# Splitting the Fourier phase's small matmuls along the columns of the TensorE array, with b1's term as a further row

## The chip, the cores and the metric

The kernel runs on one core of one Trainium2 chip. The metric is the device time of one execution in microseconds (us), taken as the median of three runs. The engines are named as in the profile: PE (TensorE, matmul), PEld (its weight load), DVE (VectorE), ACT (ScalarE), POOL (GpSimd) and SP (SyncE, which issues nearly all transfers here).

## The reference

The input has 64 samples of 96 channels and 56 by 56 places. A first layer normalizes groups, makes a 7x7 kernel for every channel with a small MLP and convolves with it. The second layer is the one that matters here. For each sample it takes the 3136 places as tokens t, and computes:

```
h = relu(bn1(layernorm(t) @ w1.T))            # 3136 tokens x 192 channels
X = fft(h, axis=tokens)                       # ortho
xr = relu(X.real*rd - X.imag*idg + rb)        # rd, idg: diagonals of r and i
xi = relu(X.imag*rd + X.real*idg + ib)
y = ifft(xr + 1j*xi).real
t = t + bn2(y @ w2.T)
t = t + ffn(layernorm(t))                     # 96 -> 384 -> 96, products in fp8
```

## The kernel before

The convolution phase (`conv_layer`) runs first and leaves its result `x1` in DRAM. Then `fourier_layer` works through the 64 samples. Each sample passes three parts.

`front` goes through seven chunks of 448 tokens. It loads tokens (`t`), sums squares, multiplies by w1 (`w1c`), normalizes and applies the ReLU into `g`, and makes the first half of the transform with `dft1`. The result goes to DRAM (`turned`).

`middle` does what the change touches. It works on 30 frequencies of the first transform (29 of them used), in four batches of 8, 8, 8 and 6 (`k0` is the batch's first, `n` its number). `load` fetches `Y`, with 112 rows (real and imaginary parts of 56 places along w), up to eight frequencies and 192 channels. `group(q)` makes the transform over w with `dft2`. For q = 0 the channels are 0 to 127, and each frequency is one matmul with 128 columns of weights (Y is the operand that is loaded, dft2 the one that streams, 112 elements). For q = 1 they are channels 128 to 191, two frequencies side by side in the upper and lower 64 partitions, each a matmul of 64 columns. Frequency 0 of the whole transform gets b1's term: a second matmul, with `b1row` (one row) as weights and `dc` streaming, is accumulated onto the first. Several ACT, DVE and POOL steps then apply the complex product and the ReLUs and leave `CD0` and `CD1` (tiles of 120 columns: 56 values, 8 zeros, 56 values). `project` multiplies them by w2: `w2b` for q = 1 in the upper or lower 64 rows of the array, `w2a` for q = 0 with all rows. Both load 120 columns of CD as weights and stream the 96 columns of w2. They accumulate into two PSUM banks, one for each h. `over_k2` transforms back over the second index with `inv1`, and the result goes to DRAM.

`ending` transforms back over the first index with `inv2` (tile `U`), adds the residual, normalizes again, and runs the MLP (`W1T`, `W2T`) on chunks of 448.

The order of all this isn't written by hand. Every step is given to a `Plan` with a due time, an engine, a cost in us, what it reads and writes, and for PE a kind (how the array is tiled). `emit` plays these costs through as events and issues each step when it starts an engine in that play, earliest due time first, favouring a step of the kind that the engine has just done within a patience of 37.3, and charging 0.13 for a change of kind. The eight PSUM banks are given out in the same play: `ps` takes one and `big` takes two together. `Pinned` then holds every engine to the order in which its steps were issued, so all engines and SP's queue are in order.

Two steps carry the costs that the change edits:

```
pe(T - 429.9, (0.92 if q else 1.9) * ng / 8 + dc_, dft, ...)
pe(T - 226.2, 0.345 * n, project, ..., kind=("halves", "full"))
```

Almost every instruction is recorded under one line of a helper (L406), so rows in the profile are told apart by their tiles: `l_psum<-dft,Y` is the transform over w, `l_psum<-dc,b1row` b1's term, `l_psum<-w2b,CD` and `l_psum<-w2a,CD` the product with w2.

Of the kernel before, what the change touches and what calls it, by code (L numbers as in the profile page):

```python
# [118 lines left out]
def constants():  # L119

    h, k = place_of_h(), np.arange(K1)
    keep = (k < NK).astype(float)
    dft1 = np.zeros((2, 64, HALF, 64))
    inv2 = np.zeros((2, 2, K1, HALF, 2, S))
    weight = keep * np.where((k == 0) | (k == NK - 1), 0.5, 1.0)

    order = np.concatenate([k[at : at + 8][h::2] for at in range(0, K1, 8) for h in range(2)])
    for wp in range(2):
        for j in range(HALF):
            w = columns()[wp, j]  # L130
            th = 2 * np.pi * k[None, :] * (S * h[:, None] + w) / HW

            dft1[wp, :S, j, :K1] = np.cos(th) / S * keep
            dft1[wp, :S, j, K1 : 2 * K1] = -np.sin(th) / S * keep

            co, si = ((f(th) / S * weight).T[order] for f in (np.cos, np.sin))
            if j == 0:
                inv2[0, wp, :, j, wp], inv2[1, wp, :, j, wp] = co, -si  # L140
            else:
                sign = 1 - 2 * wp
                inv2[0, 0, :, j, wp], inv2[0, 1, :, j, wp] = co, -sign * si
                inv2[1, 0, :, j, wp], inv2[1, 1, :, j, wp] = -si, sign * co
    a = np.arange(S)
    ph = 2 * np.pi * (a[:, None] * a[None, :]) / S
    co, si = np.cos(ph), np.sin(ph)

    dft2 = np.block([[co, -si], [si, co]]).reshape(2, S, RI)[:, place_of_w()]


    inv1 = np.zeros((2, 64, HALF, 2))
    inv1[:, :S, :, 0] = co[:, :HALF]
    inv1[0, :S, :, 1], inv1[1, :S, :, 1] = si[:, :HALF], -si[:, :HALF]
    inv1[:, :S, 0, 1] = co[:, HALF]
    inv1 = np.concatenate([inv1.reshape(128, S), np.zeros((128, 64 - S))], 1)

    dc = np.zeros((1, RI))
    dc[0, 0] = S


    f = np.arange(32)
    there = (f <= L // 2).astype(float)
    th = 2 * np.pi * (a[:, None] - (S - 1) / 2) * f[None, :] / L
    fwd_y = np.zeros((2, 64, 2, 32))
    fwd_y[:, :S, 0] = np.cos(th) * there
    fwd_y[:, :S, 1] = -np.sin(th) * there


    g = np.arange(64)  # L170
    here = (g < L).astype(float)
    half = np.arange(HALF)
    th = 2 * np.pi * (half[:, None] - (S - 1) / 2) * g[None, :] / L
    cx, sx = np.cos(th) * here, np.sin(th) * here
    fwd_x = np.zeros((2, 64, 64))
    fwd_x[0, :S] = np.concatenate([cx, sx])
    fwd_x[1, :S] = np.concatenate([cx, -sx])

    inv_x = np.tile(fwd_x.transpose(2, 0, 1), (2, 1, 1))


    share = there * np.where((f == 0) | (f == L // 2), 1.0, 2.0) / L**2
    th = 2 * np.pi * f[:, None] * (half[None, :] - (S - 1) / 2) / L
    cy, sy = np.cos(th) * share[:, None], np.sin(th) * share[:, None]
    inv_y = np.stack([np.stack(v, 1) for v in ((cy, cy), (cy, -cy), (-sy, -sy), (-sy, sy))])


    d = np.arange(KS) - RAD
    spec = np.zeros((2, 2, 32, 4, 2, 2, 64))
    for q in range(4):  # L190
        for g_ in range(2):
            for p in range(2):
                for e in range(2):
                    fy = 8 * q + 4 * e + 2 * g_ + p
                    ph = 2 * np.pi * (fy * d[:, None, None] + g * d[None, :, None]) / L
                    ph = ph.reshape(KS * KS, 64)[PAIRS:]
                    spec[p, 0, : PAIRS + 1, q, g_, e] = np.cos(ph) * here * there[fy]
                    spec[p, 1, : PAIRS + 1, q, g_, e] = np.sin(ph) * here * there[fy]

    fold = np.zeros((2, 64, 2, 64))  # L200
    fold[:, :, 0] = fold[0, :, 1] = np.eye(64) / 2.0
    fold[1, :, 1] = -np.eye(64) / 2.0
    middle = np.zeros((3, 128))
    middle[2, [0, 64]] = 1.0
    group = np.kron(np.eye(ROWS // 3), np.full((3, 3), 1.0 / 3.0))
    mean = np.full((C, C), 1.0 / C)

    sel = np.zeros((4, 32, 4))
    sel[:, 0] = np.eye(4)
    named = dict(  # L210
        dft1=dft1.reshape(128, HALF, 64), sel=sel.reshape(128, 4), dft2=dft2.reshape(RI, RI), inv1=inv1[:TOK],
        inv2=inv2.reshape(4 * K1, HALF, RI), dc=dc, group=group, center=np.eye(C) - mean,
        fwd_y=fwd_y.reshape(128, 64)[:TOK], fwd_x=fwd_x.reshape(128, 64)[:TOK], inv_x=inv_x, inv_y=inv_y.reshape(128, S),
        spec=spec.reshape(128, 4, 2, 128), middle=middle,
        fold=fold.reshape(128, 128),
        ident=np.eye(128),
    )
    return {k: np.ascontiguousarray(v, np.float32) for k, v in named.items()}
# [993 lines left out]
def fourier_layer(tc, nc, x1, out, weights, con):  # L1212
# [8 lines left out]
    with ExitStack() as ctx:  # L1221
# [17 lines left out]
            return t  # L1239

        sel, dft1 = const("sel", [128, 4]), const("dft1", [128, HALF, 64])
        dft2, inv1 = const("dft2", [RI, RI]), const("inv1", [TOK, 64])
        dc, inv2 = const("dc", [1, RI]), const("inv2", [4 * K1, HALF, RI])
        eps = cp.tile([128, 1], F32, name="eps")
        nc.vector.memset(eps, 1e-5)
        over = cp.tile([C, 32], F32, name="over")
# [7 lines left out]
        for t in CDs[0] + CDs[1]:  # L1254
# [4 lines left out]
                "w1c", "nb1", "b1row", "w2a", "w2b", "bias2", "pa", "W1T", "W2T", "fb1", "fb2",  # L1259
            )  # L1260
        )

        def pe(when, cost, step, **kw):
            plan.add(when, "PE", cost, step, lag=PE_LAG, **kw)
# [153 lines left out]
        def middle(b, T, turned):  # L1418
# [4 lines left out]
            def batch(m, T):  # L1423
# [4 lines left out]
                    return (tag, "m", b, m, *more)  # L1428

                def load():  # L1430
                    v["Y"] = sbuf("Y", [RI, 8, H1], F32, f"Y{b}_{m}")
                    for r in range(2):
                        for half in range(2):
                            p = r * S + half * HALF
                            nc.sync.dma_start(
                                v["Y"][p : p + HALF, :n], rows[half, r, :, k0 : k0 + n]
                            )

                def group(q, T):
# [6 lines left out]
                    def dft():  # L1446
                        w["ps"] = bank(ps, 2 - q).rearrange("p (g x) -> p g x", x=128)
                        for g in range(ng):
                            for e in range(1 + q):
                                k = g if q == 0 else 2 * g + e  # L1450
                                lo, hi = (64 * e, 64 * e + 64) if q else (0, 128)
                                channels = slice(128 * q, 128 + 64 * q)
                                to_ = w["ps"][lo:hi, g, :RI]
                                nc.tensor.matmul(
                                    to_, v["Y"][:, k, channels], dft2,
                                    start=True, stop=k0 + k > 0,
                                )
                                if k0 + k == 0:
                                    nc.tensor.matmul(
                                        to_, b1row[:, channels], dc, start=False, stop=True  # L1460
                                    )
                        w["re"], w["im"] = w["ps"][:, :ng, :S], w["ps"][:, :ng, S:RI]

                    def act(key, src, func, **kw):
# [18 lines left out]
                    def minus():  # L1483
# [6 lines left out]
                    )  # L1490
                    CD = nm(f"CD{q}")
                    add = plan.add
                    dc_ = 0.4 if k0 == 0 else 0.0
                    pe(T - 429.9, (0.92 if q else 1.9) * ng / 8 + dc_, dft, r=[nm("Y")],
                       w=[ps, p, r2, t, w2, CD], kind=("columns2" if q else "full"))


                    add(T - 240.9, "ACT", 0.26 + 0.84 * e,
# [17 lines left out]
                def project():  # L1516

                    for h in range(2):
                        v["o", h] = bank(nm("ps", 0, h))[:TOK]


                    for g in range(n // 2):
                        for h in range(2):
                            half = slice(64 * h, 64 * h + 64)
                            nc.tensor.matmul(
                                v["o", h][:, g * C : (g + 1) * C], v[1][half, g], w2b[half],
                                start=g == 0, stop=False,
                            )
                    ks = [k for k in range(n) if k0 + k < NK]
                    for k in ks:  # L1530
                        g, h = k // 2, k % 2
                        nc.tensor.matmul(
                            v["o", h][:, g * C : (g + 1) * C], v[0][:, k], w2a,
                            start=False, stop=k + 2 not in ks,
                        )

                width = n // 2 * C

# [34 lines left out]
                    [nm(x, y, h) for h in range(2)]  # L1573
                    for x, y in (("ps", 0), ("E", 0), ("ps", 1), ("t2", 0))
                )
                pe(T - 226.2, 0.345 * n, project, r=[nm("CD0"), nm("CD1")], w=[*o, *E], kind=("halves", "full"))
                for h in range(2):
                    U = T + 15 + 2.0 * h
                    add(U - 239.2, "ACT", 0.17 + 0.042 * n, lambda h=h: keep(h),
# [304 lines left out]
```

## Time and profile before

| what | value |
|---|---|
| median of 3 runs | 6957.5 us (6955.31 to 6960.29) |
| span of the profiled execution | 6947.6 us |
| time of the profiled execution beside its span | not given apart; the median is 9.9 us over the span |
| one sample in the steady part of the Fourier phase | 65.42 us |
| busy over the span | PE 95%, PEld 63%, DVE 75%, ACT 63%, POOL 48% |
| mean granted TensorE clock | 0.978 |

The span is the time from the first to the last instruction of one profiled execution. Busy time is the union of an engine's instructions; matmuls overlap each other and their ends are modelled, so a count of passes and the distance between starts say more of PE than its busy share. A float32 matmul stands as two passes in the trace, so x16 is eight matmuls. PEld runs beside PE. A row of the timeline merges neighbouring instructions of the same tiles: it shows the start, the time to the last one's end, the tiles, the shapes and the number, and the idle time ahead of it where there was some.

### The profile page before, as it was taken

What the parts mean: (1) busy time and instruction counts of PE and PEld (TensorE: products, weight loads), DVE (VectorE), ACT (ScalarE), POOL (GpSimd) and SP (SyncE); (2) the same over time, 40 slices, a digit from 0 to 9 for tenths busy, and PEclk for the clock granted to TensorE, in tenths of its full rate; (3) what the DMA queues carried; (4) which work ended last, traced back from release to release, by engine and by line L of the source; (5) the groups of instructions that cost most, each with busy time, mean ns of one, the idle gap of its engine ahead of it and who ended that gap; (6) DMA issues with size and microseconds to landing.
All of it is one profiled execution on the core that took longest, in us unless ns stands there. A gap on an engine that the chain in (4) does not pass through costs nothing.

```text
span 6947.6 us, 180667 instructions
## 1 busy us (share of the span) xinstructions
PE 6579.9 (95%) x67027; PEld 4382.2 (63%) x67027; DVE 5231.0 (75%) x10600; ACT 4391.6 (63%) x10582; POOL 3307.1 (48%) x3604
## 2 busy tenths in 40 slices
PE   8999999999999998999999999999999999999997
PEld 3455555555555556777777777777777777777774
DVE  4555555555555543899999999999999999999997
ACT  3444444443443433777777777877878777777776
POOL 0221111112111221666666666666666666666666
PEclk9999999999999986999999999999999999999997
DMA  4677777777777776667777767767777777677664
GB/s 138 179 200 204 207 199 204 201 198 211 199 200 200 205 195 168 184 193 195 198 191 195 194 191 195 195 192 198 193 193 198 192 194 198 190 194 197 193 183 129
DMA packets 1328576, 1334.92 MB, mean 192 GB/s; under 512 B 756763, under 2 KB 1201758, under 8 KB 1320665
## 3 DMA queue, kind: packets, MB, share of 16 engines
q1 hardware_dynamic: 1325864, 1313.79, 69.1%
q8 instruction: 532, 8.72, 0.5%
q10 hardware_dynamic: 1833, 9.57, 0.4%
q14 instruction: 347, 2.84, 0.1%
HBM read 743.17 MB, written 579.63 MB: 190 GB/s over the span
## 4 chain that ended last, share of the span: by engine, by line
DVE 27%; PE 19%; ACT 8%; issue 5%; DMA 4%; SPq 1%; POOL 0%; DVEq 0%; POOLq 0%; ACTq 0%
PE l_psum L406 17%; DVE h L406 5%; DVE CD L406 5%; DVE g L406 4%; DVE mr L406 3%; DVE x L406 3%; DVE t L406 3%; ACT h L406 3%; ACT r L406 2%; DMA turned<-t 2%; DVE p L406 2%; DVE w L406 1%; ACT t L406 1%; ACT p L406 1%; PE s L406 1%
## 5 line engine op out<-in xcount | busy, mean ns | idle before, releaser
L406 POOL TENSOR_TENSOR t<-t,t 128x504 f32<-128x504 f32 (+1 forms) x392 | 489.9, 1253 | 2105.1 <-DVE t L406 2104.8
L406 PE MATMUL pm<-w0g,xT 128*126 128x512 f32 (+3 forms) x2450 | 1151.0, 611 | 3.0 <-ACT xT L406 3.0
L406 PEld LDWEIGHTS pm<-w0g,xT 128*126 128x126 f32 (+3 forms) x2450 | 442.2, 192 | 531.5 <-issue 523.4
L406 PE MATMUL l_psum<-dft,Y 112*128 112x112 f32 (+1 forms) x7552 | 738.7, 274 | 8.3 <-ACT E L406 1.7
L406 POOL TENSOR_TENSOR t<-t,y 96x448 f32<-96x448 f32 x448 | 500.2, 1117 | 479.0 <-DVE y L406 478.8
L406 PEld LDWEIGHTS l_psum<-dft,Y 112*128 112x128 f32 (+1 forms) x7552 | 650.3, 164 | 110.0 <-DVE g L406 32.8
L406 ACT COPY B<-s 120x504 f32<-120x504 f32 (+1 forms) x392 | 207.5, 580 | 801.4 <-PE s L406 734.6
L406 PE MATMUL l_psum<-w1c,t 96*56 96x193 f32 (+1 forms) x7168 | 690.5, 336 | 0.0
L406 ACT CAST h<-l_psum 128x448 f16<-128x448 f32 x1344 | 661.2, 550 | 11.3 <-PE l_psum L406 11.3
L406 ACT COPY t<-l_psum 128x384 f32<-128x384 f32 (+2 forms) x1408 | 614.0, 486 | 29.3 <-PE l_psum L406 23.2
L406 DVE SCALAR_TENSOR_TENSOR g<-l_psum,st,nb 120x192 f32<-120x192 f32 x1792 | 627.6, 402 | 4.8
L406 DVE TENSOR_TENSOR t<-s,W 128x504 f32<-128x504 f32 (+1 forms) x784 | 481.6, 672 | 186.9 <-PE s L406 186.8
L406 POOL TENSOR_TENSOR sq<-t 96x448 f32<-96x448 f32 x448 | 476.8, 1070 | 264.5 <-PE l_psum L406 223.2
L406 POOL TENSOR_TENSOR mr<-mr 128x112 f32<-128x112 f32 x896 | 499.2, 560 | 216.8 <-ACT mr L406 179.3
L406 POOL TENSOR_TENSOR nb<-t,nb 96x448 f32<-96x448 f32 x448 | 571.8, 1277 | 56.6 <-DMA nb<-norms 56.4
L406 ACT ACTIVATE h<-h,fb 128x448 f16<-128x448 f16 x896 | 593.7, 693 | 0.0
L406 POOL TENSOR_TENSOR sqb<-t 96x448 f32<-96x448 f32 x448 | 557.7, 1255 | 41.2 <-DVE t L406 25.7
L406 PEld LDWEIGHTS l_psum<-w1c,t 96*56 96x56 f32 (+1 forms) x7168 | 505.8, 136 | 37.9 <-ACT t L406 0.3
L406 PEld LDWEIGHTS s<-inv_y,V 64*126 64x126 f32 (+1 forms) x5488 | 357.8, 194 | 229.1 <-ACT B L406 100.5
L406 PE MATMUL s<-inv_y,V 64*126 64x56 f32 (+1 forms) x5488 | 395.8, 282 | 98.6 <-ACT B L406 50.3
L406 ACT ACTIVATE t<-l_psum,pa 128x224 f32<-128x224 f32 (+3 forms) x512 | 306.4, 610 | 254.9 <-PE l_psum L406 253.1
L406 DVE TENSOR_TENSOR x<-nb 96x448 fp8e5<-96x448 f32 x448 | 362.0, 808 | 124.3 <-POOL nb L406 121.9
(131 smaller groups left out, 14058.2 us busy)
## 6 DMA issues: line engine op xcount, KB each, us to landing
turned<-t SPq DMA_DIRECT2D x896, 180.0 KB
nb<-norms SPq DMA_DIRECT2D x448, 336.0 KB
Y<-turned SPq DMA_DIRECT2D x768, 168.0 KB
Y<-turn_x SPq DMA_DIRECT2D x768, 110.2 KB
turn_y<-B SPq DMA_DIRECT2D x768, 110.2 KB
V<-turn_y SPq DMA_DIRECT2D x336, 252.0 KB
U<-turned SPq DMA_DIRECT2D x896, 90.0 KB
t<-x SPq DMA_DIRECT2D x448, 168.0 KB
```

Of the source, the lines that this page charges most:

```text
L406: ins = issue(*args, **kw)
```

## The change

The transform for q = 0 becomes two matmuls of 64 columns for each frequency, one for channels 0 to 63 into PSUM partitions 0 to 63, one for 64 to 127 into the others; q = 1 stays as it was. b1's row is put into partition 112 of Y at its first frequency, and `dc` becomes the 113th row of dft2; for frequency 0 the matmul takes 113 rows and the accumulated second matmul goes. So that the row stays, Y is no tile of the pool any more but one of two constant tiles, `Ys`, used in turn, whose row is filled once at the start of the phase from ACT's queue. In `project` each matmul is cut into columns 0 to 63 and 64 to 119. The costs and kinds given to the plan follow; due times stay.

```diff
-    dft2 = np.block([[co, -si], [si, co]]).reshape(2, S, RI)[:, place_of_w()]
+    dft2 = np.block([[co, -si], [si, co]]).reshape(2, S, RI)[:, place_of_w()].reshape(RI, RI)
...
-        dft2=dft2.reshape(RI, RI)
+        dft2=np.concatenate([dft2, dc])
...
-        dft2, inv1 = const("dft2", [RI, RI]), const("inv1", [TOK, 64])
-        dc, inv2 = const("dc", [1, RI]), const("inv2", [4 * K1, HALF, RI])
+        dft2, inv1 = const("dft2", [RI + 1, RI]), const("inv1", [TOK, 64])
+        inv2 = const("inv2", [4 * K1, HALF, RI])
...
+        Ys = [cp.tile([RI + 1, 8, H1], F32, name=f"Y{e}") for e in range(2)]
+        for t in Ys:
+            nc.scalar.dma_start(t[RI:, 0], b1row)
...
-                    v["Y"] = sbuf("Y", [RI, 8, H1], F32, f"Y{b}_{m}")
+                    v["Y"] = Ys[(4 * b + m) % 2]
...
-                            for e in range(1 + q):
-                                k = g if q == 0 else 2 * g + e
-                                lo, hi = (64 * e, 64 * e + 64) if q else (0, 128)
-                                channels = slice(128 * q, 128 + 64 * q)
-                                to_ = w["ps"][lo:hi, g, :RI]
+                            for e in range(2):
+                                k = 2 * g + e if q else g
+                                at = 128 if q else 64 * e
+                                rows_ = RI + (k0 + k == 0)
                                 nc.tensor.matmul(
-                                    to_, v["Y"][:, k, channels], dft2,
-                                    start=True, stop=k0 + k > 0,
+                                    w["ps"][64 * e : 64 * e + 64, g, :RI],
+                                    v["Y"][:rows_, k, at : at + 64], dft2[:rows_],
+                                    start=True, stop=True,
                                 )
-                                if k0 + k == 0:
-                                    nc.tensor.matmul(
-                                        to_, b1row[:, channels], dc, start=False, stop=True
-                                    )
...
-                    dc_ = 0.4 if k0 == 0 else 0.0
-                    pe(T - 429.9, (0.92 if q else 1.9) * ng / 8 + dc_, dft, r=[nm("Y")],
-                       w=[ps, p, r2, t, w2, CD], kind=("columns2" if q else "full"))
+                    pe(T - 429.9, 0.21 * ng, dft, r=[nm("Y")], w=[ps, p, r2, t, w2, CD],
+                       kind="columns2")
...
+                    cut = [slice(0, 64), slice(64, TOK)]
                     for g in range(n // 2):
                         for h in range(2):
                             half = slice(64 * h, 64 * h + 64)
-                            nc.tensor.matmul(
-                                v["o", h][:, g * C : (g + 1) * C], v[1][half, g], w2b[half],
-                                start=g == 0, stop=False,
-                            )
+                            for to in cut:
+                                nc.tensor.matmul(
+                                    v["o", h][to, g * C : (g + 1) * C], v[1][half, g, to],
+                                    w2b[half], start=g == 0, stop=False,
+                                )
...
-                        nc.tensor.matmul(
-                            v["o", h][:, g * C : (g + 1) * C], v[0][:, k], w2a,
-                            start=False, stop=k + 2 not in ks,
-                        )
+                        for to in cut:
+                            nc.tensor.matmul(
+                                v["o", h][to, g * C : (g + 1) * C], v[0][:, k, to], w2a,
+                                start=False, stop=k + 2 not in ks,
+                            )
...
-                pe(T - 226.2, 0.345 * n, project, r=[nm("CD0"), nm("CD1")], w=[*o, *E], kind=("halves", "full"))
+                pe(T - 226.2, 0.27 * n, project, r=[nm("CD0"), nm("CD1")], w=[*o, *E],
+                   kind=("quarters", "columns2"))
```

More of the change, by code (lines that the diff above doesn't have):

```diff
@@ L210, in constants @@
     named = dict(
-        dft1=dft1.reshape(128, HALF, 64), sel=sel.reshape(128, 4), dft2=dft2.reshape(RI, RI), inv1=inv1[:TOK],
-        inv2=inv2.reshape(4 * K1, HALF, RI), dc=dc, group=group, center=np.eye(C) - mean,
+        dft1=dft1.reshape(128, HALF, 64), sel=sel.reshape(128, 4), dft2=np.concatenate([dft2, dc]), inv1=inv1[:TOK],
+        inv2=inv2.reshape(4 * K1, HALF, RI), group=group, center=np.eye(C) - mean,
         fwd_y=fwd_y.reshape(128, 64)[:TOK], fwd_x=fwd_x.reshape(128, 64)[:TOK], inv_x=inv_x, inv_y=inv_y.reshape(128, S),
```

## The prediction

> **What bounds the kernel now.** I read the page's slices first, because the change touches only the second of two phases, and then the busy times of one repeating sample inside that phase.
>
> ```profile
> PE   8999999999999998999999999999999999999997
> DVE  4555555555555543899999999999999999999997
> POOL 0221111112111221666666666666666666666666
> PEclk9999999999999986999999999999999999999997
> ```
>
> Each digit is a fortieth of the span, about 174 us. From the sixteenth slice on the Fourier phase runs: PE stays at 9, and DVE climbs from 5 to 9. The clock is full there, so no gain or loss can come through the clock. The starts of its matmuls put the phase at 2661 to about 6920 us. Inside it the timeline repeats every 65.42 us, once a sample; I take one such stretch and the next:
>
> ```profile
> core 0: us, PE busy (x) PEld busy (x) DVE busy (x) ACT busy (x) POOL busy (x), PEclk, DMA share, GB/s
> 4315.28:4380.70 65.42, 62.68 (x791) 47.26 (x791) 59.93 (x125) 51.85 (x139) 43.91 (x51) 1.00 0.71 191
> 4380.70:4446.12 65.42, 62.68 (x790) 47.26 (x790) 59.91 (x125) 51.86 (x139) 43.87 (x51) 1.00 0.73 195
> ```
>
> TensorE (PE) is the fullest at 62.68 us of 65.42, but VectorE (DVE) comes close behind at 59.93. Thus two engines bound this phase. The waits of DVE in the same sample add up to 5.3 us, and the chain of waits of that sample lies on PE for 31.8%, 20.8 us, and on DVE for most of the rest:
>
> ```profile
> DVE x L406 <- POOL nb L406: 1.6, 1, 1.6
> DVE t L406 <- ACT r L406: 1.0, 2, 0.6
> DVE p L406 <- ACT r L406: 0.8, 1, 0.8
> DVE w L406 <- ACT p L406: 0.7, 1, 0.7
> ```
>
> DVE waits for POOL and ACT, which in turn wait for PE's results. The matmuls concerned are these (start, time to the modelled end, count of passes; each float32 matmul shows as two passes):
>
> ```profile
> 4322.89 0.47 PE L406 MATMUL l_psum<-dft,Y 112*128 112x112 f32 x2
> 4323.29 0.47 PE L406 MATMUL l_psum<-dc,b1row 1*128 1x112 f32 x2
> 4323.69 2.15 PE L406 MATMUL l_psum<-dft,Y 112*128 112x112 f32 x16
> 4325.77 0.40 PE L406 MATMUL l_psum<-dc,b1row 1*64 1x112 f32 x2
> 4326.10 0.98 PE L406 MATMUL l_psum<-dft,Y 112*64 112x112 f32 x14
> ...
> 4335.68 0.87 PE L406 MATMUL l_psum<-w2b,CD 64*120 64x96 f32 x12
> 4336.48 1.29 PE L406 MATMUL l_psum<-w2a,CD 128*120 128x96 f32 x10
> ...
> 4354.39 1.92 PE L406 MATMUL l_psum<-w2a,CD 128*120 128x96 f32 x16
> 4356.15 0.73 PE L406 MATMUL l_psum<-h,W2T 128*96 128x448 fp8e5 x3
> 4356.71 2.85 PE L406 MATMUL l_psum<-dft,Y 112*128 112x112 f32 x32
> 4359.50 0.77 PE L406 MATMUL l_psum<-h,W2T 128*96 128x448 fp8e5 x3
> ```
>
> **What the Trainium skill says.** The page "TensorE: Matmul & The Clock Gate", section "LDWEIGHTS (loading the stationary operand)", puts a weight load at its columns divided by 1.2 ns, whatever the rows. The trace agrees: w2a with 120 columns takes (1.92 − 1.29)/6 = 0.105 us a pass, close to 100 ns, though only 96 elements stream. The page "TensorEngine Tiling (Array Packing)", section "Key Properties", says that tiles load and multiply in parallel and that a change of tiling mode drains the engine. Here two 64-column passes of the transform start 7 ns apart and the next pair 95 ns later (single starts of the burst at 4341.49), and a burst followed by another mode holds PE about 0.09 us longer. The first page also gives a floor of about 25 ns between starts (section "Wait — 56ns, not 53.3ns?"). Four-tile bursts of the column sums (96*32, 112 streamed) stand here at 95 ns for four, 24 ns each, with 7 ns between starts inside the four; a hard floor isn't seen, but 82 ns for four hasn't been seen either.
>
> **The change part by part.** I call a round the passes that run side by side. A round costs the longer of its load and its stream. Streaming 112 elements takes 95 ns and 193 take 163.5 (w1c, same view), so 0.84 ns an element, and 96 elements should take 82 ns. That is an estimate from these two.
>
> *Product with w2b.* Now two row halves of 120 columns make a round of 105 ns: (0.87 us for x12 against 1.08 for x16, 4 passes, 2 rounds). A full batch has 8 rounds. Afterwards four 64-by-64 tiles make a round, there are twice as many passes and still 8 rounds, at 82 ns: −0.18 us. The bounds are nothing gained (a floor of 25 ns gives 100 ns a round) and −0.18.
>
> *Product with w2a.* Now 16 passes of 105 ns. Afterwards 32 passes in 16 rounds of two column tiles at 82 ns: −0.37 us. Together −0.55 us for each of three batches and 23 ns times 6 + 10 rounds = −0.37 us for the short fourth: −2.0 us a sample.
>
> *Transform over w, channels 0 to 127.* Now 58 passes a sample (29 frequencies) at 111.5 ns (single starts), the load of 128 columns. Afterwards 58 rounds of two at 95 ns: −0.94 us. Channels 128 to 191 were split already.
>
> *b1's term.* It needs an accumulation onto the matmul just before it, and PE runs these one after another. The first batch of the sample takes 4322.89 to 4327.01 = 4.12 us, an ordinary one 4356.71 to 4359.50 = 2.79 us, so the two extra matmuls cost 1.33 us. As a 113th row they cost nothing: load and stream don't depend on rows, and both are within 128. −1.33 us.
>
> *Mode changes.* In the built program's order of instructions PE changes its tiling 44.9 times a sample before and 47.7 after: 2.8 times 0.09 = +0.25 us.
>
> *Loads and buffers.* One constant of 448 bytes goes, two copies of b1row (768 bytes each) are sent once from ACT's queue, behind the constants of that phase; dft2 gets a row. b1row is made in the convolution phase. What hides these is the load of inv2 (1470 KB) ahead of them on the same queue; uncovered, some 2 us each and once, by the 2.14 us that the chain shows for a store of the output. Y keeps its two buffers, its four loads a batch and SP's order of kinds, so SP and POOL are passed by nothing. DVE, ACT and POOL get no instruction more or less; their steps only move in order.
>
> The sum on PE is −2.0 − 0.94 − 1.33 + 0.25 = −4.0 us a sample, −257 us over 64. From 62.68, PE falls to 58.7 us, below DVE's 59.93. **DVE becomes the fuller engine**, so not all arrives. If relief counted only where the chain lies on PE, 31.8% of 4.0 = 1.3 us would arrive; if all of it, 4.0. DVE can't go under 59.93, which would be −5.5. Against it stands the order: the scheduler fills every engine's queue from the costs given to it, and in the built program before, the order of PE repeats exactly from the third sample to the sixtieth, while after, nearly every sample has another order, with a sample's work in 36 to 82 bursts where before it was 62. An irregular order on in-order queues makes late arrivals likelier for a DVE at 92%. I take 1.5 us a sample: DVE 59.93 busy of 63.9, 94%. 64 × 1.5 = 96 us.
>
> The profiled span is 6947.6 us; the median of the runs is 9.9 us more, and no view shows other time around the span. The change is made against the span: 6947.6 − 96 + 9.9 = 6861.
>
> **The rivals.** *First: everything arrives.* PE was the fullest engine and its 4.0 us come off each sample: 61.4 us, 6957.5 − 257 = 6700. For it: only 2.7 us a sample of PE are idle now. Against it: DVE would have to be 97.6% busy, with waits of 1.5 us where it has 5.3.
>
> *Second: slower.* The new order costs DVE more in late arrivals than PE gives back. The place is DVE's queue in the Fourier phase: its waits for ACT, POOL and PE. It decides from 5.5 us of DVE waits a sample, that is once DVE is under 91.6% busy. At 90% the sample takes 66.6 us, +1.2 × 64 = +77: 7034. For it: the irregular order; DVE instructions also lengthen beside POOL (the fp16 add and max on 128x448 has a mean of 0.93 us, though the fp16 add on 96x448 stands in the timeline once with 0.33 and once with 1.03), and another order may line them up worse. Against it: PE has 4 us of new slack, which absorbs lateness.
>
> *Third: the split doesn't pay.* If two 64-column loads ran one after the other, a round would take some 2 × 53 = 107 ns: w2a and the transform would gain 4 ns or lose 2, w2b nothing, and only b1's term would go: −1.33 + 0.25 = −1.1 us on PE, of which the chain's share of 31.8% arrives, 0.34 us: 6957 − 22 = 6935. Against it: pairs at 95 ns in this trace.
>
> **How the numbers follow.** First case, DVE takes over: 0.56, from 0.5 to 2.6 us a sample, 6790 to 6926. Everything arrives: 0.13. Slower: 0.21. Split doesn't pay: 0.10, with part of it, 0.04 in all, inside 0.2%, which is about what a measurement of this kernel can tell from no change (14 us). Faster 0.75, same 0.04, slower 0.21. The range leaves out the farther half of the first rival and the far end of the second: 6730 to 6995. The case's own range is 6790 to 6926.
>
> **What would show it.** In the profile after: w2a bursts of 32 passes in about 1.4 us and w2b of 32 in about 0.83 us to the next burst; no rows with dc; PE under 59.5 us a sample and DVE over 93% busy. If w2b takes 1.0 us, the floor holds. If PE's busy time has fallen by 4 us and DVE's waits have grown over 5.5 us a sample, the second rival is right. The forecast is wrong if PE stays over 61 us of work, or if DVE is over 96% busy.

## The result and the profile after

The change is faster, but by little: 6935.6 us (6924.4 to 6943.6, 6 runs) against 6958.9 us (6952.2 to 6974.3, 6 runs of the kernel before), a ratio of 0.996 with a 95% interval of 0.9944 to 0.9975. The direction was forecast, the size was not: 23 us of the 96 forecast came. The number lies inside the whole stated range (6730 to 6995), but outside the range of the favoured case (6790 to 6926).

The profiled span is 6935.9 us, 12 us under that of before; the time of that execution is 1.8 us over its span, so most of the 9.9 us by which the median of before lies over its span is that the profile shows one of its faster executions. These are the slices of the page after, the rows that answer to those shown of before:

```profile
PE   8999999999999997999999999998999999999997
DVE  4555555555555544898999989989889989899987
POOL 0221121121211121676676767666666666667766
PEclk9999999999999997999999999999999999999998
```

DVE no longer stands at 9 throughout; it changes between 8 and 9. PE has one slice with 8 in the phase. PEclk reads 9 as before: at 174 us a slice and nine tenths a digit, the row is too coarse for what follows. The busy times of 3900 us inside that phase, first before and then after (the columns are those of the row of headings):

```profile
core 0: us, PE busy (x) PEld busy (x) DVE busy (x) ACT busy (x) POOL busy (x), PEclk, DMA share, GB/s
2800.00:6700.00 3900.00, 3736.07 (x47072) 2815.16 (x47070) 3563.12 (x7381) 3084.78 (x8211) 2623.05 (x2977) 1.00 0.72 194
```

```profile
2800.00:6700.00 3900.00, 3593.38 (x57095) 2613.27 (x57087) 3519.59 (x7363) 3064.09 (x8197) 2645.11 (x2976) 0.98 0.71 194
```

PE's busy time fell by 143 us in that stretch, and DVE was busy for less of the same time too. So PE was relieved and nobody used the room. The last stores of the samples in the trace give the time of one sample. In the kernel before it is 65.48 us. In the change single samples take 41 to 94 us, and the mean over some fifty of them is 65.46 to 65.77 us, depending on which are taken. So the steady part became no faster; what was gained came mostly at the start of the phase, whose first ten samples end 791 us after its first matmul (before: 811).

The matmuls themselves are what they should be. A piece of the timeline of the change comes first, then one of a kernel with the same matmuls in the order of before (e1 below):

```profile
3726.91 0.77 PE L406 MATMUL l_psum<-h,W2T 128*96 128x448 fp8e5 x3
3727.60 2.52 PE L406 MATMUL l_psum<-dft,Y 112*64 112x112 f32 x48
3730.05 0.88 PE L406 MATMUL l_psum<-g,dft 56*64 56x192 f32 x16
```

```profile
4344.18 0.89 PE L406 MATMUL l_psum<-w2b,CD 64*64 64x96 f32 x32
4345.00 1.53 PE L406 MATMUL l_psum<-w2a,CD 128*64 128x96 f32 x32
4346.54 0.77 PE L406 MATMUL l_psum<-h,W2T 128*96 128x448 fp8e5 x3
```

The whole transform of a batch (48 passes) takes 2.45 us to the next row, where it took 2.79. w2b takes 0.82 us, w2a at best 1.37 us and here, ahead of another mode, 1.54. No row with dc is left.

What is new is this. The windows of one stretch of the change (11, 10 and 10 us) and the timeline of the middle one:

```profile
3704.00:3715.00 11.00, 9.06 (x115) 6.14 (x111) 10.17 (x18) 7.28 (x21) 7.49 (x9) 1.00 0.81 235
3715.00:3725.00 10.00, 10.00 (x68) 5.66 (x65) 7.48 (x17) 6.44 (x17) 9.05 (x11) 0.50 0.39 110
3725.00:3735.00 10.00, 9.67 (x171) 6.85 (x171) 6.74 (x14) 7.91 (x19) 4.53 (x6) 0.99 0.66 174
```

```profile
3715.44 1.30 PE L406 MATMUL l_psum<-x,W1T 96*128 96x448 fp8e5 x3
3716.68 0.60 PE L406 MATMUL l_psum<-sq,over 96*32 96x112 f32 x8
3717.21 1.36 PE L406 MATMUL l_psum<-h,W2T 128*96 128x448 fp8e5 x3
```

After a stretch in which PE was busy for only 9.06 of 11 us, the granted clock is 0.50 for 10 us, PE is "100% busy", and three passes of W2T take 1.36 us where at full clock they take 0.77. A busy share of 10.00 is a slow engine here, not a full one. The clock records of the trace add up to 188 us of half clock between 2800 and 6700 us, and to none in the kernel before. The bursts in them took longer than the same bursts' medians at full clock: 60 us in all if only bursts that lie wholly inside are counted, 88 us if all that touch them are. This is an estimate; if everything in those 188 us took twice its time, it would be 94 us.

### The profile page after: what moved, and what is told of

Read it like the earlier page. It is cut to its first block, busy times and chain, and to the rows that moved or that the text cites. A ratio compares the mean times of both kernels' runs of the same rounds, so it can differ in the third digit from the quotient of the medians.

```text
span 6935.9 us, 202441 instructions
## 1 busy us (share of the span) xinstructions
PE 6416.9 (93%) x78035; PEld 4167.4 (60%) x78035; DVE 5187.9 (75%) x10600; ACT 4374.4 (63%) x10582; POOL 3325.4 (48%) x3604
## 4 chain that ended last, share of the span: by engine, by line
DVE 16%; PE 16%; ACT 8%; DMA 7%; POOL 7%; issue 5%; SPq 1%; POOLq 0%; ACTq 0%; DVEq 0%
PE l_psum L406 16%; ACT h L406 3%; DVE CD L406 3%; DVE g L406 2%; DVE h L406 2%; DVE t L406 2%; POOL mr L406 2%; ACT t L406 2%; DMA nb<-norms 2%; DMA turned<-t 2%; DMA Y<-turned 1%; DVE w L406 1%; POOL sqb L406 1%; DVE x L406 1%; POOL nb L406 1%
## 5 line engine op out<-in xcount | busy, mean ns | idle before, releaser
L406 POOL TENSOR_TENSOR nb<-t,nb 96x448 f32<-96x448 f32 x448 | 591.5, 1324 | 126.5 <-DMA nb<-norms 119.9
L406 PE MATMUL l_psum<-dft,Y 112*64 112x112 f32 (+1 forms) x11264 | 623.1, 263 | 15.5 <-DVE g L406 7.5
L406 POOL TENSOR_TENSOR sq<-t 96x448 f32<-96x448 f32 x448 | 502.8, 1128 | 271.6 <-PE l_psum L406 219.4
L406 PEld LDWEIGHTS l_psum<-dft,Y 112*64 112x64 f32 (+1 forms) x11264 | 552.6, 137 | 99.2 <-issue 36.3
L406 POOL TENSOR_TENSOR sqb<-t 96x448 f32<-96x448 f32 x448 | 516.3, 1158 | 169.7 <-DVE t L406 131.3
L406 POOL TENSOR_TENSOR mr<-mr 128x112 f32<-128x112 f32 x896 | 521.6, 585 | 148.3 <-ACT mr L406 110.2
L406 POOL TENSOR_SCALAR w<-w 128x448 f32<-128x448 f32 (+3 forms) x512 | 244.1, 480 | 518.0 <-DVE w L406 499.4
L406 PE MATMUL l_psum<-inv,U 120*96 120x112 f32 x3584 | 440.7, 270 | 46.4 <-ACT t L406 18.4
```

Source lines behind the costliest of these rows:

```text
L406: ins = issue(*args, **kw)
```

## The experiments

Every ratio is to runs of the kernel before on the same chip, with its 95% interval. The first four separate the matmuls from the order. The plan's costs and kinds make the order; so the change's matmuls can be issued in the order of before, and the old matmuls in the change's order.

**e1, the matmuls in the order of before.**

```diff
-                    pe(T - 429.9, 0.21 * ng, dft, r=[nm("Y")], w=[ps, p, r2, t, w2, CD],
-                       kind="columns2")
+                    dc_ = 0.4 if k0 == 0 else 0.0
+                    pe(T - 429.9, (0.92 if q else 1.9) * ng / 8 + dc_, dft, r=[nm("Y")],
+                       w=[ps, p, r2, t, w2, CD], kind=("columns2" if q else "full"))
...
-                pe(T - 226.2, 0.27 * n, project, ..., kind=("quarters", "columns2"))
+                pe(T - 226.2, 0.345 * n, project, ..., kind=("halves", "full"))
```

> All matmul edits of the change, but the plan's costs and kinds as before, so that every engine keeps the order of before (one that repeats every sample). Order theory (the faster matmuls are worth something, the irregular order takes it back): clearly faster than the change, 1.5 to 3 us less a sample than before, so 6770 to 6865 us. DVE theory (VectorE bounds the phase whatever the order, so faster matmuls are worth little): 6930 to 6950 us, like the change.

Measured: 6881.3 us, ratio 0.9889 (0.9874 to 0.9904), 77 us less than before and 54 less than the change. A sample takes 64.31 us.

**e2, the order without the matmuls**: the reverse of that edit, on the kernel before.

> The matmuls of before with the plan's costs and kinds of the change, so that the engines follow the change's order with the slow matmuls. Order theory: the order costs about what e1_matmuls_only gains beyond the change, so slower than before by 70 to 150 us: 7030 to 7110. DVE theory: within 30 us of before, 6930 to 6990.

Measured: 7059.7 us, ratio 1.0147 (1.0133 to 1.0161), 102 us more. A sample takes 67.26 to 67.55 us, depending on which are taken.

So the change is the sum of a gain and a loss that the same diff makes. The matmuls are worth 77 us in the old order and 124 us (7059.7 to 6935.6) in the new; the order costs 102 us with the old matmuls and 54 with the new. The DVE theory's numbers hold in neither run. The order theory's hold in e2; e1 is clearly faster than the change, as that theory has it, but lies 16 us above its range: the matmuls are worth less than it had them.

**e3 and e4, parts of the matmuls in the order of before.** e3 has e1 with `cut = [slice(0, TOK)]`, so that only the transform and b1's term are changed; e4 is before with the change's `project` alone.

> Only the transform's split and b1's term as a row, in the order of before; the product with w2 is as before. By the prediction's sizes 0.94 + 1.33 of 4.3 us of matmul time go, so about half of the gain of e1_matmuls_only under the order theory: 6870 to 6920. Under the DVE theory nothing to 10 us: 6945 to 6960.

> Only the product with w2 is cut along the columns, in the order of before; transform and b1's term as before. 2.0 of 4.3 us of matmul time go, so about half of the gain of e1_matmuls_only under the order theory: 6870 to 6920. Under the DVE theory nothing to 10 us: 6945 to 6960.

Measured: e3 6896.3, ratio 0.991 (0.9895 to 0.9924), 63 us; e4 6921.7, ratio 0.9944 (0.9931 to 0.9956), 39 us. e3 lies in its range, e4 2 us beyond it. Together they would be 102 us; e1, which has both, gives 77.

**e8, b1's row alone.**

```diff
-                                nc.tensor.matmul(
-                                    to_, v["Y"][:, k, channels], dft2,
-                                    start=True, stop=k0 + k > 0,
-                                )
-                                if k0 + k == 0:
-                                    nc.tensor.matmul(
-                                        to_, b1row[:, channels], dc, start=False, stop=True
-                                    )
+                                rows_ = RI + (k0 + k == 0)
+                                nc.tensor.matmul(
+                                    to_, v["Y"][:rows_, k, channels], dft2[:rows_],
+                                    start=True, stop=True,
+                                )
```

> Only b1's term as a 113th row, nothing split, order of before. 1.33 us of PE a sample go by the prediction. If the chain's share of a third arrives: 6958 - 0.42 x 64 = about 6930. If all arrives: 6873. If b1's term is hidden: 6950 to 6960.

Measured: 6910.7, ratio 0.9936 (0.992 to 0.9952), 45 us. That is between the two forecasts of a third and of all. The smallest edit is thus worth more than half of what all the matmul edits give in this order.

**e5 and e6, other orders from the change's own costs.** The plan was played through with moved due times and another patience, and one order that repeats every sample was taken, and one that doesn't. The edits are of the kind `add(T - 424.2, ...)` to `add(T - 519.2, ...)`.

> The change with its costs and kinds, but other due times for 11 steps and a patience of 51, so that the built order repeats every sample from the ninth on; PE changes its tiling 42.0 times a sample (47.7 in the change). Regularity theory (an order that does not repeat costs the change about what it loses against e1_matmuls_only): as fast as e1_matmuls_only or faster, 6800 to 6885 us, with little time at half clock. DVE theory: VectorE stays near 61 us busy a sample, so not under 6870. Theory that the change's costs given to the plan are wrong and any order made from them is poor: 6920 to 6960.

> The same as e5_regular_order in kind: the change's costs and kinds with other due times (22 steps, patience 26.9), but chosen so that the order still does not repeat; PE changes its tiling 47.5 times a sample. Regularity theory: near the change, 6910 to 6960 us, with 100 us or more at half clock in the phase. Theory that only this one order of the change is unlucky: like e1_matmuls_only or better, 6830 to 6885.

Measured: e5 6920.3, ratio 0.9945 (0.9931 to 0.9959); e6 6932.3, ratio 0.9964 (0.9954 to 0.9973). The repeating order has little half clock (31 us against 123), and is still 39 us behind e1. Repetition isn't what the order of before has over the others; my theory of it fell here. What remained was the third one, that the change's costs are bad for the plan.

**e9, the same moved due times with the costs and kinds of before.**

> The matmuls of the change with the plan's costs and kinds of before, but with the due times and the patience of e5_regular_order: a third order that repeats every sample (from the fourteenth on), with 47.5 changes of tiling a sample. Cost theory (what spoils the order is the change's costs and kinds in the plan): near e1_matmuls_only, 6870 to 6900 us. Theory that the one order of before suits the engines and any other order, repeating or not, loses: 6915 to 6980.

> The matmuls of the change with the plan's costs and kinds of before and the due times and patience of e6_other_irregular_order: this order repeats only every seventh sample, with 51.3 changes of tiling a sample. Cost theory: 6870 to 6900 us. Theory that any order but that of before loses: 6930 to 7000, with 50 to 150 us at half clock.

Measured: with e5's due times 7022.7, ratio 1.0077 (1.0054 to 1.01), and with e6's 6985.7, ratio 1.0031 (1.0019 to 1.0043). Both are slower than before, with faster matmuls, and the first of them repeats every sample; it is slower than either theory had it. Under these due times the old costs are worse than the new ones by 92 and 47 us (from the ratios), under the due times of before they are better by 54. So neither set of costs is good or bad in itself; costs and due times act together. The moved due times had been picked with the new costs, which may be why the old ones do badly there. With six orders measured for the same matmuls, from 6881 to 7023 us, the spread between orders is larger than all that the matmuls bring.

Two things grow with the time over these six, by and large; both are taken between 2800 and 6700 us of the profiled execution:

| order | median us | profiled execution us | waits of DVE us | half clock us |
|---|---|---|---|---|
| e1 | 6881 | 6880 | 260 | 14 |
| e5 | 6920 | 6918 | 315 | 31 |
| e6 | 6932 | 6911 | 330 | 123 |
| the change | 6936 | 6938 | 363 | 188 |
| e9, due times of e6 | 6986 | 7000 | 381 | 246 |
| e9, due times of e5 | 7023 | 7023 | 470 | 236 |

That the waits of DVE grow is no explanation yet: DVE has the same instructions in all six, so a longer sample must show as more waiting unless its instructions lengthen. The half clock could be a cause. If work in it takes twice its time at most, as estimated above, half of the half-clock time is the most that is lost. That can't explain e5 (31 us of it against 14, but 39 us slower than e1); the change it could (174 us more of it, so up to 87, and 54 us slower). In all but one of the six the largest single wait of DVE is for ACT. First e1, then the last e9 (what waited, for whom, us in total, times, longest):

```profile
DVE x L406 <- POOL nb L406: 80.3, 59, 2.8
DVE p L406 <- ACT r L406: 47.5, 60, 0.8
DVE t L406 <- ACT r L406: 47.4, 120, 0.4
```

```profile
DVE p L406 <- ACT r L406: 81.5, 106, 0.8
DVE mr L406 <- ACT mr L406: 73.6, 117, 3.6
DVE w L406 <- ACT t L406: 69.8, 54, 5.0
```

**e7 and e10, PE's lulls filled.** Both are the change in its own order with useless matmuls; e7 has this one in each down projection, e10 has as many of them as fit, in the same form, ahead of each step that stood after an idle time:

```diff
+                    nc.tensor.matmul(
+                        v["m2", c][:, :HID2], W1T[:, 0, :C],
+                        W1T.rearrange("p a b -> p (a b)"), start=True, stop=True,
+                    )
```

> The change with one useless fp8 matmul (96x96 weights, 384 streamed) ahead of each MLP down projection, into the bank that the projection overwrites, 7 a sample, so that PE has something to do in one of its most frequent waits; some 0.2 us each, 1.4 us a sample of added PE work. Clock theory (the lulls of the irregular order drop PE's clock to half, 191 us of the phase, and this is most of the loss): half-clock time falls under 100 us and the time falls by 10 to 40 us, to 6895 to 6925. Lateness theory (the loss is the engines waiting for each other, the clock only follows): the same or slower, 6935 to 7000, whatever the clock.

> The change in its own order with 1104 useless fp8 matmuls (96x96 weights, 384 streamed) put ahead of just the 243 steps of PE that stand after an idle time over 0.4 us in the profile of the change (217 us in all), as many as the idle time holds. Clock theory (PE's lulls put it at half clock for 188 us of the phase, and this makes the irregular order dear): half-clock time falls under 80 us and the time falls by 20 to 60 us, to 6875 to 6915. Lateness theory: half-clock time may fall, but the time stays within 10 us of the change or grows up to 7000.

Measured: e7 6934.0, ratio 0.9969 (0.9959 to 0.9979), with 147 us at half clock instead of 188; too small a step to tell the theories apart. e10 6987.3, ratio 1.0037 (1.0024 to 1.0049), with 96 us at half clock. Half of the slow time went and the kernel became 52 us slower; PE's busy time in that stretch rose by 89 us. But e10 filled the lulls badly: of the 208 us in which PE still stands idle there, 124 us stand ahead of useless matmuls themselves, so these ran only after the lull. So the clock's part in the loss is open. For it speaks that in the change 179 of its 188 half-clock us lie in PE's part of the chain of waits, so by that chain the slowed matmuls were then what the rest waited for.

**e11 to e13, less work on DVE.** The MLP's bias is added on 8 of 448 columns (`y = v["y16", c][:, :8]`), in e1, in before and in the change.

> e1_matmuls_only with the fb2 bias added on the first 8 of 448 columns only (left out on the other 440), which takes about 0.35 us from each of 7 VectorE instructions a sample, 2.4 us a sample, 157 us in all; order unchanged. If VectorE's own work sets the pace with the fast matmuls: most of it arrives, 6881 - (90 to 157) = 6725 to 6790. If its waits for other engines set it: under a third arrives, 6830 to 6881.

> Before with the same bias left out on 440 of 448 columns. If PE sets the pace here: under a third of 157 us arrives, 6905 to 6959. If VectorE sets it already before the change: most of it, 6800 to 6870.

> The change with the same bias left out on 440 of 448 columns. If VectorE's work sets the pace in the irregular order too: 6780 to 6845. If lateness of the other engines sets it: under a third of 157 us arrives, 6885 to 6936.

Measured: 6862.8, ratio 0.9866 (0.9846 to 0.9887); 6927.7, ratio 0.9959 (0.9944 to 0.9974); 6910.1, ratio 0.9932 (0.9916 to 0.9949). These tell less than meant. The instruction went from 440 ns to 317 ns on average, no further, so 55 us were taken out, not 157. Of these, 18 to 31 us arrived in each, for e11 no more than the noise (its interval overlaps that of e1).

**e14, e16 and e17, cleaner cuts.** e14 is e1 with one of three ReLUs on ACT cut short, e16 is e1 and e17 is before with the residual add on DVE cut short (`t = t[:, :8]`).

> e1_matmuls_only with the first of the MLP's three ReLUs applied to 8 of 448 columns (left out on the rest), which takes about 0.45 us from each of 7 ACT instructions a sample, some 3.2 us a sample, 200 us in all; order unchanged. If ACT sets the pace: over half arrives, under 6780. If VectorE's own work sets it: nothing to 30 us, 6850 to 6885. If the engines wait for each other in turn and none sets it: a tenth to a third, 6815 to 6860.

> e1_matmuls_only with the residual add of the ending on 8 of 448 columns (left out on the rest), which takes about 0.5 us from each of 7 VectorE instructions a sample, 3.5 to 4 us a sample, 220 to 260 us in all; order unchanged. If VectorE's own work sets the pace with the fast matmuls: over half arrives, under 6760. If no engine alone sets it: a tenth to a third, 6795 to 6860.

> Before with the same residual add on 8 of 448 columns. If PE sets the pace there: a third at most, 6880 to 6958. If VectorE sets it already: over half, under 6840.

Measured: e14 6891.1, ratio 0.989 (0.9873 to 0.9907); e16 6886.2, ratio 0.9887 (0.9871 to 0.9903); e17 6938.8, ratio 0.9962 (0.9948 to 0.9975). The residual fell from 672 ns to 214 ns, 3.2 us a sample and 205 us in all. Of these, nothing arrived in e16 (e1 has 0.9889) and 27 us in e17. Of ACT's 2.6 us a sample in e14 nothing arrived either. e17 was forecast, e14 and e16 fell below what was forecast for engines that wait in turn. The half clock blurs these two: it is 92 us in e14 and 75 in e16 against 14 in e1, which can have cost 39 and 31 us at most. The windows of e1 and then of e16 show where it went:

```profile
2800.00:6700.00 3900.00, 3587.03 (x58351) 2601.09 (x58352) 3629.59 (x7512) 3119.71 (x8354) 2664.81 (x3027) 1.00 0.70 197
```

```profile
2800.00:6700.00 3900.00, 3598.76 (x58094) 2604.79 (x58084) 3366.67 (x7475) 3087.61 (x8315) 2687.17 (x3016) 0.99 0.71 197
```

DVE's busy share falls from 93% to 86%, PE stays at 92%, and the time stands still. DVE's busy time is 263 us less, 193 of them the residual's and some 60 those of another instruction, the fp16 `h<-h,fb`, whose mean fell from 962 to 817 ns. They are waits now: DVE's waits rose from 260 to 521 us, with POOL's `nb` first:

```profile
DVE x L406 <- POOL nb L406: 194.9, 119, 4.8
DVE h L406 <- ACT h L406: 107.5, 182, 2.2
```

So neither DVE's nor ACT's own work alone sets the pace of e1: over half of what was taken out should then have arrived. That a chain sets it which goes from one engine to the next fits this, but isn't shown. No run takes further work from POOL, for which DVE waits longest here, or from PE in e1.

## Why the prediction was right and wrong

*The sizes of the matmuls* held. w2b was forecast at 0.83 us and takes 0.82; w2a at 1.4 and takes 1.37 to 1.54; the rounds of the split transform were forecast at 95 ns and stand at 96 (the second pass starts 7 ns after the first, the next pair 89 ns later). b1's rows are gone. Four tiles of 96 elements did run in 82 to 83 ns (20.7 ns a pass), so the bound of 25 ns a start did not appear. What the Trainium skill's "TensorEngine Tiling (Array Packing)", section "Key Properties", says of tiles that load and multiply in parallel is right here too: four 64-by-64 tiles take 82 to 83 ns where two tiles of 64 by 120 took 105.

*What arrives without the order* was nearly right. The chain's share (31.8% of 4.0) gave 1.3 us a sample as the lower end; e1 gives 1.17 us (65.48 to 64.31). For the parts the same share gives 27, 41 and 46 us for e8, e4 and e3; measured are 45, 39 and 63. It is a rough guide for PE, not a law: the cut of w2's product gives 39 us alone and 14 on top of e3. For DVE it fails: the lines of e1's chain below have DVE at 45%, and of 205 us taken from it in e16 nothing came. Over the same 3900 us the chain of waits lies on PE for 27.0% before, 12.2% in e1 and 26.8% in the change:

```profile
by line: PE l_psum L406 27.0%; DVE h L406 8.7%; issue 8.6%; DVE CD L406 8.1%; DVE g L406 6.9%; DVE mr L406 5.1%; DVE x L406 4.9%; DVE t L406 4.7%; ACT h L406 4.3%; ACT r L406 2.9%; DMA turned<-t 2.6%; DVE p L406 2.6%; DVE w L406 2.3%; ACT t
```

```profile
by line: PE l_psum L406 12.2%; issue 9.9%; DVE CD L406 9.5%; DVE h L406 8.9%; ACT h L406 7.4%; DVE g L406 6.4%; DVE t L406 5.5%; DVE x L406 4.1%; DVE mr L406 3.8%; DVE p L406 3.7%; ACT r L406 3.6%; DVE w L406 3.0%; DMA turned<-t 2.6%; ACT t
```

```profile
by line: PE l_psum L406 26.8%; issue 7.5%; DVE CD L406 4.4%; DVE g L406 4.3%; ACT h L406 4.1%; DVE h L406 4.0%; POOL mr L406 3.3%; DVE t L406 3.3%; DMA nb<-norms 3.1%; ACT t L406 3.1%; DMA turned<-t 2.8%; DMA Y<-turned 2.6%; DVE w L406 2.5%
```

PE hasn't as much to do in the change as before, and yet the chain lies on it as long. It has 1044 us of PE there and 474 in e1; 165 of these 570 us more stand in half clock, the rest isn't explained.

*The step that failed* is "I take 1.5 us a sample". 23/64 = 0.4 us arrived. The irregular order had been seen and named, but in the sum its cost was put at nothing: it stood only in the choice of 1.5 between 1.3 and 4.0, above what e1 later showed with no loss of order at all. In its place belongs a term of its own: e1's 1.2 us less 0.8 us (54/64) for the order with these matmuls; e2 puts it at 1.6 us (102/64) with the old matmuls. The second rival named this mechanism, but not its size: the order took back 54 of 77 us, not more than PE gave. Its mark of 5.5 us of DVE waits a sample was hardly a mark, since before has 327 us in 3900, also 5.5 a sample; in the change there are 6.1. PE is at some 60.4 us of a sample (92% of 3900 us) and DVE at 90%: neither the marks of a right forecast came (under 59.5 us, over 93%) nor those of a wrong one (over 61 us, over 96%). Both looked for work on one engine, and the loss is idle and slowed time.

*The clock* was excluded with "no gain or loss can come through the clock". That held for the order of before; 188 us at half clock in the change say otherwise. It isn't the relief of PE that brings them but the order: e1, with the same matmuls, has 14 us, and e2, with the old ones, 140.

*"DVE becomes the fuller engine"* is right as a count in e1 (3629.6 us of DVE to 3587.0 of PE), not in the change (3519.6 to 3593.4), and wrong as a cause: e16 takes 3.2 us a sample off DVE and gains nothing. *Everything arrives* was wrong, as forecast. *The split doesn't pay* gave 6935 us, which is what was measured, but by chance: its rounds of 107 ns did not come, they are 82 to 96 ns.

What stays open is what in the order of before makes it better than the five others. Repetition isn't enough (e5, e9), nor are its costs without its due times (e9). It has the fewest waits of DVE and the least half clock; how much of the loss is the clock's, and which placement brings either, isn't shown. The fastest kernel of these that computes everything is e1: the change's matmuls with the plan's costs left as they were, 6881 us, 1.1% faster than before.

## What to carry to other kernels

Where a planner turns costs into an order, a better matmul and its new cost are two changes: measure the matmul in the old order first, then the order with the old matmul. The chain's share was nearer to what a relief of PE brought than PE's busy time was, but failed for DVE; so try it with one experiment before relying on it. Give a new order a term of its own, for which 1 to 2% is the scale here. A busy share of 10.00 in a window with a granted clock of 0.50 is a loss, so read both columns together.

## What the runs showed of the hardware

*The clock changes on a grid of 3.41 us, and falls after a cell of it with much idle time.* Half clock doesn't follow from PE's idle time in all. Between 2800 and 6700 us, before has 148 us idle, in pieces under 1.5 us, and no half clock; e2 has 168 us and 140 us of half clock; e1 has 307 us, with 71 pieces over 1 us, 61 of them ahead of W2T, and 14 us of half clock. The clock records show what counts. In each of the nineteen traces all changes of the granted clock lie, within 10 ns, on a grid of 3.41 us. Between 2800 and 6700 us there are 270 drops to 0.50 in all. In the cell of the grid just before a drop PE was busy for 72.2% of the time at most, by its modelled ends. Of the cells at full clock, all 114 with PE busy for under 46.6% were followed by a drop, and none of the 20148 over 72.2% was; of the 963 between, 156 were. So what counts is the idle time that falls into one cell, not the length of a piece; what decides between 46.6 and 72.2% isn't shown. The pieces can be short. Ahead of the drop at 3714.92 us, in the windows above, they were these two:

```profile
3712.47 0.40 PE L406 MATMUL l_psum<-sqb,over 96*32 96x112 f32 x8 [0.61 <-POOL sqb L406]
3713.32 0.40 PE L406 MATMUL l_psum<-sq,over 96*32 96x112 f32 x8 [0.45 <-DVE t L406]
```

The page "TensorE: Matmul & The Clock Gate" of the Trainium skill, section "HAM oscillation — how this bites in real kernels", tells of gaps over some 3.4 us; here idle pieces shorter than that, close together, went ahead of it.

*The same DVE instruction takes longer beside POOL.* The fp16 add `y<-y,fb` on 448 columns took 319 ns on average in e1 where no POOL instruction ran beside it, and 598 ns where one did. On 8 columns (e11) it took 212 and 454 ns. Cutting 98% of the columns thus took only 123 ns off the mean of 440. The fp16 `h<-h,fb` took 244 ns on average in e1 without POOL, never over 336, and 1088 ns with it. The float32 residual add doesn't show this: 661 ns without and 667 ns with POOL in the change.
